# Where three products of the first double read their left operands, and when two weight chunks are loaded

## Chip, cores and metric

The kernel runs on one core of one Trainium2 chip. The metric is the device time of one execution in microseconds (us). Everything is in 32-bit floats.

## What is computed

The input `x` is 4 batches of 1024 tokens with 1024 features. A self-attention layer with 16 heads of 64 is applied with a residual, and then a causal convolution over tokens with 4 taps, also with a residual. Cut to what matters:

```python
scale, shift = split(emb @ W_emb + b_emb)
xn = rms_norm(x, g_norm) * (1 + scale) + shift
q, k, v = heads(xn @ W_qkv)                 # 1024 x 3072 weights
q, k = rms_norm(q, g_q), rms_norm(k, g_k)
o = softmax(q @ k.T / 8) @ v                # per head
x = x + o + o @ W_out
x = x + causal_conv(x, taps=cond) + b       # 4 taps per feature
```

## The kernel before

**Products.** `xn @ W_qkv` is the work around the change. It is computed as 2 by 2 block products with seven multiplications in place of eight (a Strassen scheme). The left blocks are the two token halves by the two feature halves of `xn`, A11, A12, A21, A22, and four sums of them: S1 = A21 + A22, S2 = S1 - A11, S3 = A11 - A21, S4 = A12 - S2. The right blocks are two head pairs' weights by feature halves and four differences T1 to T4. The products are named P1 (A11), P2 (A12), P6 (S2, T2), P7 (S3, T3), P4 (A22, T4), P5 (S1, T1) and P3 (S4). One run of the scheme serves two head pairs and is called a `Double`; there are 4 per batch, 16 in all. Each of its seven products has four token tiles `t` = 0 to 3 of 128 tokens, so a double has 28 pieces (`piece`, L634). A piece is four matmuls over `k` = 0 to 3 into one PSUM tile, followed by adds on VectorE (DVE) or a copy on ScalarE (ACT). The PSUM tiles come from a pool of three (`ps_m`, tag "m"), which transposes share.

**Left operands.** A left operand is needed transposed: features on partitions. `Chunk` (L259) makes all of them for one feature block `k` and one token quarter `q` (tiles 0, 1 for q = 0 and tiles 2, 3 for q = 1): transposes on TensorE, scale and shift on ACT or DVE, the four sums on DVE (`sums`, L318, records at L321). They stand in one or several SBUF tiles, reached by `self.r(place)`, and `store` (L336, records at L338) writes them to a DRAM scratch `scrA[b][q]`. A product reads its operand back with `load_a` (L610, records at L620) into one of three buffers of tag "a". For batch 0 the eight chunks' tiles lie in SBUF room that other things use later (`R_HOMES`, L249): the second quarter's `k` = 1 in the pool "x", and its `k` = 2 and 3 in the two tiles of the pool "ob".

**The first double.** P1 and P2 of the first double get their operands from `direct` (L622) and the first of the chunks are made meanwhile. Its order of pieces is `FIRST_PRODUCTS` (L573): P1 and P2 on all tiles, then P6, P7, P4 on tiles 0 and 1 (pieces 8 to 13), P6, P7, P4 on tiles 2 and 3 (pieces 14 to 19), P5 (20 to 23), P3 (24 to 27). For tiles 0 and 1, `load_a` returns at once and `piece` takes the operand from the chunk's own tiles; for tiles 2 and 3 it is read back from `scrA`.

**Right operands.** `Weights` (L524) loads four blocks of `W_qkv` for one `k` into one tile of the pool "ob" (or elsewhere for the first double), makes the differences (`combine`, L553, records at L561: GpSimd for the first double, DVE later) and stores them to the DRAM scratch `scrB` (L562). They are made once, in batch 0. `STEPS_B` (L1084) says at which pieces of a double the four chunks of the next double are loaded; the first tuple is that of the first double. For the second double's chunks 0 and 1 the differences follow 12 us after the load on the kernel's own clock (`TO_B`), for later ones in a gap. `load_w` (L592) fetches a product's right operand, from `scrB` (L604) or from `W_qkv` (L601), into one of three buffers of tag "w".

**Order of the work.** TensorE (PE), DVE, ACT and GpSimd run their instructions in the order in which the program gives them: `piece`, `tick` and `defer` keep a clock of estimated times and put deferred steps where it says. The DMAs are all issued by SyncE (SP), whose order is made by the framework's scheduler. An SP issue that must wait, for a buffer or for data, holds those behind it.

Of the kernel before, what the change touches and what calls it, by code (L numbers as in the profile page):

```python
# [15 lines left out]
P = 128  # L16
# [5 lines left out]
def kernel(  # L22
# [42 lines left out]
    KH = NJ // 2  # L65
# [33 lines left out]
    def flush(due):  # L99
        while True:  # L100
            ready = [e for e in pending if due(e)]
            if not ready:
                return
            entry = min(ready, key=lambda e: e[:2])
            pending.remove(entry)
            entry[3]()

    def tick(us):

        clock[0] += us  # L110
        flush(lambda e: e[0] <= clock[0])
# [28 lines left out]
    def need(*key):  # L140
        flush(lambda e: e[2] == key)
# [440 lines left out]
    class Double:  # L582
# [26 lines left out]

        def load_a(self, i):  # L610

            _, place, t = self.products[2 * i]
            if (place, t // 2) in self.a or self.n == 0 and t < 2:
                return
            for k in range(KH):
                if self.b == 0:
                    need("s", t // 2, k)
                need("r", self.b, t // 2, k)
            a = self.a[place, t // 2] = self.tile_a(place, t // 2)
            nc.sync.dma_start(a, scrA[self.b][t // 2][:, place])  # L620
# [13 lines left out]
        def piece(self, i):  # L634

            name, place, t = self.products[i]
            px, py = self.pairs
            pm = ps_m.tile([P, 512], F32, tag="m", name=f"pqkv_{self.n}_{name}_{t}")[:, :W3]
            w, a = self.w[name], self.a.get((place, t // 2))
            for k in range(KH):  # L640
                if a is None:
                    need("s", 0, k)
                nc.tensor.matmul(  # L643
                    pm,
                    (chunks[0, k].r(place) if a is None else a[:, k, :])[:, t % 2 * P : (t % 2 + 1) * P],
                    w[:, k, :],
                    start=(k == 0),
                    stop=(k == KH - 1),
                )
            tick(TIME)  # L650
            if name == "P1":
                self.u2[t] = apool.tile([P, W3], F32, tag="u2", name=f"u2_{self.n}_{t}", bufs=HT)
                nc.scalar.copy(self.u2[t], pm)
            elif name == "P6":
                nc.vector.tensor_add(self.u2[t], self.u2[t], pm)
            elif name == "P7":
                self.u3[t] = apool.tile([P, W3], F32, tag="u3", name=f"u3_{self.n}_{t}", bufs=HT)
                nc.vector.tensor_add(self.u3[t], self.u2[t], pm)
            else:
                pr, g, u = {"P2": (px, 0, self.u2), "P4": (px, 1, self.u3), "P5": (py, 1, self.u3), "P3": (py, 0, self.u2)}[name]  # L660
                for dst, at in pr.parts(g * HT + t):
                    nc.vector.tensor_add(dst, u[t][:, at], pm[:, at])  # L662
                if name == "P5":
                    nc.vector.tensor_add(self.u2[t], self.u2[t], pm)
            if t == HT - 1 and name in ENDS:
                c, g = ENDS[name]
                self.pairs[c].done(g)
# [413 lines left out]
    STORE = 30.0  # L1081
    TO_B = 12.0
    P6_AT = 3
    STEPS_B = ((14, 17, 22, 25), (7, 12, 17, 22))  # L1084
    outs, norms, chunks, weights, doubles, quads = {}, {}, {}, {}, {}, {}
    LAST = (B - 1) * 2 * NJ
    NB = 2 * NJ
# [4 lines left out]
    def piece(T):  # L1092
# [17 lines left out]
        if T % 2 == 0 and 4 <= a < ND * NPR // 2:  # L1110
            free(lambda: load_a(a))
# [8 lines left out]
        if n < ND:  # L1120
# [18 lines left out]

            if b == 0 and d + 1 < PB and i in STEPS_B[d > 0]:  # L1140
                free(lambda: Weights(d + 1, STEPS_B[d > 0].index(i)).load())

# [87 lines left out]
    def between(p):  # L1230

        b, i = divmod(p, NB)
        slots = [[] for _ in range(7)]
        for j in range(7):
            T = 7 * (p + 4) + j
            slots[j] = piece(T) if T < ND * NPR + 16 else []
        slots[0].append((0.0, lambda: store(AGE)))
        d, k = divmod(p - 11, NB)
        if 0 <= d < B - 1 and k % 2 == 0 and k < NJ:
            slots[0].append((0.0, lambda: OutSums(d, k // 2).load()))  # L1240
        for a, g in enumerate(range(products_until(p), products_until(p + 1))):
            slots[(2, 5)[a]] += out_product(g)
        if p in REST_PLAN:
            at = sum(n for q, n in REST_PLAN.items() if q < p)
            for m in REST[at : at + REST_PLAN[p]]:
                slots[6] += [(0.0, lambda: store(AGE_REST))] + out_pieces(m)
                slots[6].append((0.0, lambda m=m: late.append((clock[0], outs[m].store))))
        return [piece for slot in slots for piece in slot]
# [59 lines left out]
    for T in range(NPR):  # L1308
        for step in START.get(T, ()):
            step()  # L1310
        run(piece(T))
# [87 lines left out]
```

## Time and profile before

| | |
|---|---|
| time, median of 3 runs | 2877.23 us (2870.78 to 2878.03) |
| profiled execution | 2868.63 us |
| its span, first to last instruction | 2866.9 us |
| mean granted TensorE clock | 0.995 |
| PE busy | 2766.6 us |
| DVE busy | 2183.8 us |
| ACT busy | 1689.7 us |
| DMA | 510.98 MB, 178 GB/s on the mean |

The times of rows are those of one profiled execution, counted from its first instruction. Rows of PE are matmuls (PEld the weight loads beside them); one matmul of the program is two records. "Idle before" is the engine's idle time ahead of a row with what ended it. The granted clock is the share of full speed that TensorE was given. DMA rows named SPq are the issues, not the transfers.

The first 140 us hold the start: embedding, the first operands and the first double. Attention begins with the scores of unit 0 at 136.8 us; from then on pieces of the next doubles are spread between the attention's units.

### The profile page before, as it was taken

The page shows a single profiled execution, that of the slowest core. Times are in us where ns is not written, and L with a number is a line of the kernel's source. Part 1 is how long each engine was busy: PE and PEld are TensorE (multiplying, and loading weights), DVE is VectorE, ACT ScalarE, POOL GpSimd, SP SyncE. Part 2 cuts the span into 40 slices and gives each one's busy share as a digit, 9 for nine tenths or more (in the row PEclk, how much of TensorE's full clock was granted, in tenths as well). Part 3 has the DMA queues.
Part 4 walks back from the last instruction along what each step waited for, and adds up shares of the span by engine and source line. Part 5 has one row for each costly group of instructions (what it writes and reads, how often), then busy time and mean ns, then how long its engine had stood idle before and what let it go on. Part 6 is the DMA issues. An engine that isn't in the chain of part 4 may idle for free.

```text
span 2866.9 us, 32127 instructions
## 1 busy us (share of the span) xinstructions
PE 2766.6 (97%) x10581; PEld 1310.3 (46%) x10581; DVE 2183.8 (76%) x2648; ACT 1689.7 (59%) x2278; POOL 1347.7 (47%) x534
## 2 busy tenths in 40 slices
PE   6999989999999999999999999999999999999898
PEld 3544444444444444454444444444444444444344
DVE  4488878888888777787878777777787868787863
ACT  4166757765656667764655667666565656565532
POOL 2055555565554553544554554454454455545520
PEclk9999999999999999999999999999999999999999
DMA  9954555645554565764565455675565435533333
GB/s 321 292 169 144 186 163 168 217 160 181 169 170 157 195 192 181 232 207 162 180 221 168 167 191 176 219 233 171 168 220 191 144 132 170 166 104 100 118 107 118
DMA packets 417277, 510.98 MB, mean 178 GB/s; under 512 B 40864, under 2 KB 326872, under 8 KB 407384
## 3 DMA queue, kind: packets, MB, share of 16 engines
q1 hardware_dynamic: 417112, 508.93, 54.5%
q8 instruction: 85, 1.39, 0.2%
q14 instruction: 80, 0.66, 0.1%
HBM read 413.43 MB, written 95.40 MB: 177 GB/s over the span
## 4 chain that ended last, share of the span: by engine, by line
PE 72%; DVE 13%; DMA 5%; ACT 4%; issue 3%; POOL 2%; SPq 1%; DVEq 0%; ACTq 0%; POOLq 0%
PE pqkv_P L643 28%; PE s L683 14%; PE pav L746 14%; PE po L1004 5%; PE po_P L935 4%; DVE mx L700 4%; PE po L935 3%; DVE sp L719 3%; DVE r L321 1%; POOL sum L725 1%; ACT sp L691 1%; PE qkt L502 1%; PE tot L761 1%; ACT sp L723 1%; DMA rec<-scrR 1%
## 5 line engine op out<-in xcount | busy, mean ns | idle before, releaser
L643 PE MATMUL pqkv_P<-w_P,a 128*128 128x384 f32 x3504 | 1193.0, 491 | 33.3 <-issue 10.1
L725 POOL TENSOR_TENSOR sum<-sum,sp 128x1024 f32<-128x1024 f32 x384 | 958.2, 2495 | 64.9 <-ACT sp L723 34.3
L643 PEld LDWEIGHTS pqkv_P<-w_P,a 128*128 128x128 f32 x3504 | 650.0, 191 | 507.1 <-issue 94.1
L691 ACT COPY sp<-s 128x1024 f32<-128x1024 f32 x512 | 506.2, 1016 | 461.8 <-PE s L683 415.2
L700 DVE TENSOR_TENSOR mx<-mx,sp 128x1024 f32<-128x1024 f32 x384 | 516.6, 1345 | 155.2 <-ACT sp L691 127.7
L719 DVE TENSOR_TENSOR sp<-sp,mbp 128x1024 f32<-128x1024 f32 x512 | 603.7, 1209 | 18.3 <-ACT mbp L714 18.0
L723 ACT ACTIVATE sp<-sp 128x1024 f32<-128x1024 f32 x512 | 526.7, 1054 | 140.2 <-DVE sp L719 136.3
L705 POOL PARTITION_ALL_REDUCE mb<-mx x64 | 220.5, 3446 | 817.8 <-DVE mx L700 618.0
L683 PE MATMUL s<-qT,kT 64*128 64x512 f32 x2048 | 514.1, 618 | 20.0 <-DVE sp L719 12.8
L746 PE MATMUL pav<-sp,v 128*64 128x512 f32 x2048 | 482.7, 603 | 0.0
L725 POOL TENSOR_TENSOR sum<-sp,sp 128x1024 f32<-128x1024 f32 x64 | 151.4, 2366 | 484.3 <-ACT sp L723 232.5
L683 PEld LDWEIGHTS s<-qT,kT 64*128 64x128 f32 x2048 | 174.6, 186 | 312.8 <-issue 202.9
L1040 DVE SCALAR_TENSOR_TENSOR y<-x,cols,y 128x512 f32<-128x512 f32 x192 | 248.3, 1298 | 48.4 <-ACT y L1028 43.8
L746 PEld LDWEIGHTS pav<-sp,v 128*64 128x64 f32 x2048 | 130.4, 136 | 327.2 <-issue 318.7
L700 DVE TENSOR_TENSOR mx<-sp,sp 128x1024 f32<-128x1024 f32 x64 | 107.8, 1685 | 104.1 <-ACT sp L691 104.0
L662 DVE TENSOR_TENSOR qk<-u,pqkv_P 128x256 f32<-128x256 f32 x256 | 106.0, 414 | 78.3 <-PE pqkv_P L643 76.9
L1004 PE MATMUL po<-ob,wo 128*128 128x512 f32 x352 | 155.1, 592 | 0.0
L935 PE MATMUL po_P<-o_P,wq_P 128*128 128x512 f32 x320 | 144.0, 592 | 0.4 <-DVE sp L719 0.4
L714 ACT COPY mbp<-mb 128x1024 f32<-128x1024 f32 x64 | 65.1, 1018 | 115.9 <-POOL mb L705 115.9
L494 DVE TENSOR_TENSOR qk<-qk,ms 128x1024 f32<-128x1024 f32 x64 | 126.4, 1975 | 2.2
L935 PE MATMUL po<-o_P,wq_P 128*128 128x512 f32 x240 | 108.0, 592 | 0.0
L480 ACT ACTIVATE sq<-qk 128x512 f32<-128x512 f32 x128 | 76.8, 628 | 51.0 <-DVE qk L662 51.0
(97 smaller groups left out, 1864.6 us busy)
## 6 DMA issues: line engine op xcount, KB each, us to landing
a<-scrA SPq DMA_DIRECT2D x215, 512.0 KB
w_P<-scrB SPq DMA_DIRECT2D x64, 768.0 KB
o_P<-scrS SPq DMA_DIRECT2D x40, 1024.0 KB
w_P<-in_L_cond_W_qkv_dram SPq DMA_DIRECT2D x192, 192.0 KB
o_P<-scrO SPq DMA_DIRECT2D x30, 1024.0 KB
scrA<-r SPq DMA_DIRECT2D x28, 896.0 KB
wq_P<-scrW SPq DMA_DIRECT2D x70, 256.0 KB
xc<-in_x_dram SPq DMA_DIRECT2D x64, 256.0 KB
```

What stands on the lines that cost most here:

```text
L643: nc.tensor.matmul(pm, (chunks[0, k].r(place) if a is None else a[:, k, :])[:, t % 2 * P : (t % 2 + 1) * P], w[:, k, :], start=(k == 0), s ...
L683: nc.tensor.matmul(ps[:, h, :], pr.kT[kt // HT][h * D : (h + 1) * D, kt % HT * P : (kt % HT + 1) * P], pr.qT[self.half][h * D : (h + 1) * ...
L691: nc.scalar.copy(sp, ps)
L700: nc.vector.tensor_max(self.mx, self.mx if kt > 1 else self.sp[0], self.sp[kt])
L705: nc.gpsimd.partition_all_reduce(self.mb.rearrange("p h q -> p (h q)"), self.mx.rearrange("p h q -> p (h q)"), P, bass_isa.ReduceOp.max,)
L719: nc.vector.tensor_sub(self.sp[kt], self.sp[kt], self.mb)
L723: nc.scalar.activation(sp, sp, AF.Exp)
L725: nc.gpsimd.tensor_tensor(self.sum, self.sum if kt > 1 else self.sp[0], sp, ALU.add)
L746: nc.tensor.matmul(self.pav[h * D : (h + 1) * D, :], self.pr.v[kt // HT][:, kt % HT, h * D : (h + 1) * D], self.sp[kt][:, h, :], start=(kt ...
L935: nc.tensor.matmul(pm, self.w[name][:, k, :], self.o[name][:, k, :], start=(k == 0 and name not in ("P2", "P3", "P4")), stop=(k == KH - 1),)
L1004: nc.tensor.matmul(self.pm, self.w[kh][:, k % KH, :], oTs[b, k, half], start=False, stop=(k == NJ - 1),)
L1040: nc.vector.scalar_tensor_tensor(self.y, self.x1[:, k : k + HN], cols[:, r : r + 1], self.y, ALU.mult, ALU.add)
```

## The change

Three edits. `load_a` also returns at once, in the first double, for P6, P7 and P4 on any tile. `piece` then takes the operand from the chunk of the tile's own quarter, `chunks[0, t // 2 * KH + k]` (KH is 4), and asks that the sums of that quarter have been given. `STEPS_B` loads chunks 0 and 1 of the second double at pieces 18 and 20 of the first in place of 14 and 17. P5 and P3 on tiles 2 and 3 still read from `scrA`.

```diff
         def load_a(self, i):
-            _, place, t = self.products[2 * i]
-            if (place, t // 2) in self.a or self.n == 0 and t < 2:
+            name, place, t = self.products[2 * i]
+            if (place, t // 2) in self.a or self.n == 0 and (t < 2 or name in ("P6", "P7", "P4")):
                 return
...
             for k in range(KH):
+                chunk = chunks.get((0, t // 2 * KH + k))
                 if a is None:
-                    need("s", 0, k)
+                    need("s", t // 2, k)
                 nc.tensor.matmul(
                     pm,
-                    (chunks[0, k].r(place) if a is None else a[:, k, :])[:, t % 2 * P : (t % 2 + 1) * P],
+                    (chunk.r(place) if a is None else a[:, k, :])[:, t % 2 * P : (t % 2 + 1) * P],
...
-    STEPS_B = ((14, 17, 22, 25), (7, 12, 17, 22))
+    STEPS_B = ((18, 20, 22, 25), (7, 12, 17, 22))
```

## Prediction

> **What bounds the kernel now.** I read the page's busy shares and chain first, then the waits of TensorE (PE), then the timeline of the stretch that the change touches.
>
> ```profile
> PE 2766.6 (97%) x10581; PEld 1310.3 (46%) x10581; DVE 2183.8 (76%) x2648; ACT 1689.7 (59%) x2278; POOL 1347.7 (47%) x534
> ...
> PE 72%; DVE 13%; DMA 5%; ACT 4%; issue 3%; POOL 2%; SPq 1%; DVEq 0%; ACTq 0%; POOLq 0%
> ```
>
> PE is busy 97% of the span and holds 72% of the chain, so only two things can shorten the run: PE work taken out, or PE idle time. The change takes no matmul out. Of the 100 us of PE idle, the page's waits name one that the change aims at: 5.2 us, once, for a transfer `a<-scrA`. The chain in order of time shows what made it:
>
> ```profile
> 84.74 5.74 DMA scrA<-r
> 90.50 5.23 DMA a<-scrA
> 95.86 13.47 PE pqkv_P L643 x32
> ```
>
> The last store of the second quarter's operands is issued at 84.74 and lands at about 90.5; only then may the read of the same data go out, and it is another 5.23 us before PE starts at 95.86. The timeline of PE around it (start, length, then idle before in brackets):
>
> ```profile
> 77.43 13.20 PE L643 MATMUL pqkv_P<-w_P,r 128*128 128x384 f32 x40
> 95.86 13.47 PE L643 MATMUL pqkv_P<-w_P,a 128*128 128x384 f32 x32 [5.23 <-DMA a<-scrA]
> 109.17 0.60 PE L502 MATMUL qkt<-ident,qk 128*128 128x128 f32 x4
> ...
> 145.52 10.59 PE L643 MATMUL pqkv_P<-w_P,a 128*128 128x384 f32 x32
> 155.94 0.60 PE L502 MATMUL qkt<-ident,qk 128*128 128x128 f32 x4
> ```
>
> A product of one token tile is 8 of these records. Both x32 rows are four products, yet one takes 13.47 us and the other 10.59. The stretches say why (columns: length, busy time of PE, weight load, DVE, ACT, POOL, then granted PE clock, DMA share, GB/s):
>
> ```profile
> 91.50:94.90 3.40, 0.00 (x0) 0.00 (x0) 0.00 (x0) 0.00 (x0) 0.00 (x0) 1.00 0.88 293
> 94.90:98.30 3.40, 2.44 (x4) 1.52 (x5) 0.00 (x0) 0.00 (x0) 0.00 (x0) 0.50 0.98 284
> 98.30:101.70 3.40, 3.40 (x6) 1.69 (x5) 0.34 (x1) 0.00 (x0) 0.00 (x0) 0.50 1.07 364
> 101.70:105.00 3.30, 3.30 (x12) 1.92 (x11) 0.77 (x2) 0.00 (x0) 0.00 (x0) 0.99 0.32 103
> ```
>
> After the empty stretch PE got half its clock from 94.9 to 101.7. The wait costs its idle time and a slow restart.
>
> **Part 1: the three reads of the second quarter go; the products read the tiles where they were made.** The operands are made by DVE at L321; its last one before these products ends at 84.7, and the products' weights (P6, P7, P4) are already in use for the first quarter. So P6 on token tile 2 needs nothing that is late. It would start where the fifth product after 77.43 ends. Two products take 5.16 us start to start (115.21 to 120.37), one 2.58; five of the x40 row give 77.43 + 13.20 less the row's 0.16 of overlap (5.32 against 5.16) = 90.47. Idle removed: 95.86 - 90.47 = 5.39 us.
> Slow restart removed: start to start the slow four take 109.17 - 95.86 = 13.31, the normal four 155.94 - 145.52 = 10.42; 2.89 us. [...] Here two windows were granted half clock, of which PE ran 101.7 - 95.86 = 5.84 us, half of it lost = 2.9. [...]
> The reads themselves (3 x 512 KB) also leave the DMA engines, which are at a share of 0.9 to 1.0 there. That gain is not counted: what comes later is tested below for being in time.
>
> **Part 2: the queue of SP.** The list of the built program shows the order: after the second quarter's last store come at once the three stores of the first quarter that stood at 92.42, then the reads of S1 and S4 for the second quarter (for P5 and P3), then P5's weights, the first operand of the second double, P3's weights, and only then chunk 0 and chunk 1 of the second double, each four reads. Those two chunks are written into tiles that the change now keeps in use until P4 on tile 3, so SP waits there for PE, with the second double's P1 weights, the next batch's x and the second double's P2 weights behind it. Before:
>
> ```profile
> 87.66 1.95 SPq L546 DMA_DIRECT2D b<-in_L_cond_W_qkv_dram  x3
> 90.50 1.29 SPq L620 DMA_DIRECT2D a<-scrA  x3
> ...
> 92.42 3.28 SPq L338 DMA_DIRECT2D scrA<-r  x3
> ...
> 104.20 0.34 SPq L604 DMA_DIRECT2D w_P<-scrB  x1
> ```
>
> P5's weights go out when P6 on tile 3 frees their buffer: before 104.20 for a use at 115.21; now 90.47 + 5.16 = 95.6 for a use at 106.9. The same 11 us; nothing. S1's read goes out at 90.5 behind 1.3 MB of stores and is used at 112.1; at 300 GB/s that is some 6 us; nothing. P1's weights of the second double waited for P4's buffer before as well and are used 30 us later; nothing.
> Chunk 0 goes out when P4 on tile 3 is nearly done, 90.47 + 6 x 2.58 + two transposes of 0.44 = 106.8; four issues at 0.62 end at 109.3. Landing: at best just behind the issue; at worst like the read at 90.50, which took 5.2 us under a full DMA load: 114.5. I take 112, since fewer transfers stand before it. Chunk 1 goes out behind P1's weights, 112 to 114.5, and lands by 119.7 at worst.
>
> **Part 3: DVE combines the two chunks later (L561).** The list puts chunk 0's four subtractions behind P5's second tile and the scaling of qk, in front of the adds of P5's third tile; chunk 1's behind P5's fourth tile. Durations as here:
>
> ```profile
> 118.99 2.32 DVE L561 TENSOR_TENSOR b<-b 128x384 f32<-128x384 f32 x4
> 121.23 0.41 DVE L662 TENSOR_TENSOR qk<-u,pqkv_P 128x256 f32<-128x256 f32 x1
> ```
>
> [...] So a late chunk holds up evictions. Walking it with all PE times 8.28 earlier: P5 tile 1 is evicted 112.3 to 113.3, reciprocal and scaling to 114.7, chunk 0 114.7 to 116.9 (it is there, at 112, at worst 114.5), P5 tiles 2 and 3 to 118.9, chunk 1 to 121.2, two reductions to 122.4, P3 tile 0 to 122.9. PE wants that PSUM tile back (three share the tag) at 131.12 - 8.28 = 122.8. A wait of about 0.1; bounds 0 and 1.0 (if each DVE row runs 5% longer). I take 0.1.
> From unit 0's scores on, the instruction lists of all compute engines are the same, so everything shifts as one. The next stop of PE, 2.85 us before 159.39, comes from DVE's rows behind the scores (chunks 2 and 3 among them) and shifts with it.
>
> **Sum.** -5.39 - 2.89 + 0.1 = -8.2 us. The profiled execution took 2868.6 us with a span of 2866.9; it would take 2860.4. It lies 8.6 below the median of the runs; the same 8.2 off the median gives 2869.0.
>
> **Rivals.**
> (a) More than that. The runs spread from 2870.8 to 2878.0 and the profiled one is below all; a wait on a store and a read at full DMA load is a place where an execution can lose more than 5.2 us, and without it that loss goes too. Also the half clock after the stop at 159.39 (1.9 us: 4.51 for one product) hangs on where the window falls. Against it: no row shows where the slower runs lose. It would give 10 to 16 less: about 2864.
> (b) Partly given back. P3's tile waits for the full 1.0 and chunk 0 lands some us late, or the shifted windows of the clock cost a second slow restart of 2.9. It would leave 2 to 6: about 2873.
> (c) Slower. One mechanism: chunk 0 is not there when DVE reaches it at 114.7. DVE stands, P5's adds behind it wait, PE runs out of PSUM tiles, us for us, and a stop of over 2.7 us adds a slow restart of 2.9. Landing at 120.0 uses up the gain; landing at 128.6 gives 2886, slower by 0.3%. For it: reads at 0.62 us each in one queue behind a wait for PE, and DMA shares of 0.9 to 1.0 between 80 and 140. Against it: even the 5.2 us read is in time by 0.2.
> That the change doesn't act can be left out: the list of PE reads r tiles in all six products.
>
> **How the numbers follow.** Full gain carried through 0.55 (2866 to 2872); (a) 0.25; (b) 0.09; (c) 0.11. A measurement of this kernel can tell about 0.3%, 8.6 us, from no change; the likeliest case lies at its edge, so half of it (0.28) counts as faster. Faster 0.28 + 0.25 = 0.53; within 0.27 + 0.09 = 0.36; slower 0.11. Range 2861 to 2875: all of the likeliest, most of (a) and (b).
>
> **What would show it.** Right: PE goes from r to r at about 90.5 with no idle time, the granted clock stays 1.00 from 80 to 120, six products take 16.4 us with their transposes, unit 0's scores begin at about 128.6 (before 136.82), and the shift is still 8 us at 1000 us. Part 3 right: L561 at about 114.7 and 118.9 without idle time before it, and PE's wait before P3's third tile under 1 us. Wrong: an idle DVE before L561, PE waiting for DVE there, a slow restart at another place, or a shift that fades where DVE sets the pace (180 to 860 us).

## The result and the profile after

The changed kernel took 2864.91 us (median of 6 runs, 2860.03 to 2866.47), the kernel before 2876.0 us (median of 6, 2870.48 to 2878.03). The ratio is 0.9962, with a 95% interval of 0.9948 to 0.9975: 0.38% or 11 us faster, forecast 8.2 us (0.29%). A second measurement of the same kernel, below, gave 0.9974 (0.9962 to 0.9986). The mean of the two is 9.2 us.

The page of the changed kernel (one execution of 2866.47 us, span 2864.7, clock 0.993), its busy times and the shares of the chain:

```profile
PE 2768.9 (97%) x10581; PEld 1312.7 (46%) x10581; DVE 2187.2 (76%) x2648; ACT 1689.6 (59%) x2278; POOL 1347.5 (47%) x534
...
PE 75%; DVE 11%; ACT 4%; DMA 4%; issue 2%; POOL 2%; SPq 1%; DVEq 0%; POOLq 0%; ACTq 0%
```

The instructions of the compute engines are as many as before. PE is busy 2.3 us longer (2768.9 against 2766.6), although a slow restart is gone; the section on the second trace of the kernel before comes back to that. Its share of the chain rose from 72% to 75%, and that of the DMAs fell from 5% to 4%. The chain in order of time (start, length) no longer has the store and the read in it:

```profile
78.30 23.35 PE pqkv_P L644 x72
101.65 0.44 PE qkt L502 x4
102.09 2.58 PE pqkv_P L644 x8
```

The timeline of PE around the change (start, length, then idle before in brackets):

```profile
78.14 23.52 PE L644 MATMUL pqkv_P<-w_P,r 128*128 128x384 f32 x72
101.49 0.60 PE L502 MATMUL qkt<-ident,qk 128*128 128x128 f32 x4
101.92 2.75 PE L644 MATMUL pqkv_P<-w_P,r 128*128 128x384 f32 x8
...
123.69 2.82 PE L644 MATMUL pqkv_P<-w_P,a 128*128 128x384 f32 x8
...
129.45 1.99 PE L684 MATMUL s<-qT,kT 64*128 64x512 f32 x8
```

Nine products run from one `r` tile to the next without a stop: 72 records in 23.52 us, where before there were 40, a stop and 32. From the start of this row to unit 0's scores it is 129.45 - 78.14 = 51.31 us; before, with the scores at

```profile
136.82 1.99 PE L683 MATMUL s<-qT,kT 64*128 64x512 f32 x8
```

it was 136.82 - 77.43 = 59.39. The difference, 8.08 us, is what the change does in this stretch; forecast 8.2. The granted clock in the stretch (columns: length, busy time of PE, weight load, DVE, ACT, POOL, then granted PE clock, DMA share, GB/s) is whole. The kernel before first, then the changed one:

```profile
80.00:100.00 20.00, 14.77 (x40) 8.16 (x39) 7.11 (x18) 0.00 (x0) 0.00 (x0) 0.87 0.96 321
```

```profile
80.00:100.00 20.00, 20.00 (x63) 11.64 (x63) 9.47 (x21) 0.00 (x0) 0.00 (x0) 1.00 0.93 320
100.00:120.00 20.00, 20.00 (x69) 12.06 (x68) 11.09 (x26) 4.00 (x7) 0.00 (x0) 1.00 0.85 259
```

SP's queue and the two chunks' differences on DVE went as walked:

```profile
96.52 0.32 SPq L604 DMA_DIRECT2D w_P<-scrB  x1
...
107.08 2.54 SPq L546 DMA_DIRECT2D b<-in_L_cond_W_qkv_dram  x4
109.71 2.56 SPq L601 DMA_DIRECT2D w_P<-in_L_cond_W_qkv_dram  x4
112.31 2.62 SPq L546 DMA_DIRECT2D b<-in_L_cond_W_qkv_dram  x4
```

```profile
115.31 2.33 DVE L561 TENSOR_TENSOR b<-b 128x384 f32<-128x384 f32 x4
117.56 0.41 DVE L663 TENSOR_TENSOR qk<-u,pqkv_P 128x256 f32<-128x256 f32 x1
...
119.54 2.33 DVE L561 TENSOR_TENSOR b<-b 128x384 f32<-128x384 f32 x4
```

No idle time stands ahead of either L561 row: both chunks had landed.

One thing does not fit at first sight. The two profiled executions differ by only 2.2 us in span (2866.9 and 2864.7), and instance by instance the lead shrinks: 7.4 us at the first maximum of unit 0, 4.3 at 400 us, 1.5 from 800 to 1000 us, 3.3 behind 2000 us. The prediction had named such a fading lead as a sign against it. The experiments had to settle that as well.

### The profile page after: what moved, and what is told of

It reads as the page before. It is cut to its first block, busy times and chain, and to the rows that moved or that the text cites. A ratio compares the mean times of both kernels' runs of the same rounds, so it can differ in the third digit from the quotient of the medians.

```text
span 2864.7 us, 32127 instructions
## 1 busy us (share of the span) xinstructions
PE 2768.9 (97%) x10581; PEld 1312.7 (46%) x10581; DVE 2187.2 (76%) x2648; ACT 1689.6 (59%) x2278; POOL 1347.5 (47%) x534
## 4 chain that ended last, share of the span: by engine, by line
PE 75%; DVE 11%; ACT 4%; DMA 4%; issue 2%; POOL 2%; SPq 1%; DVEq 0%; POOLq 0%; ACTq 0%
PE pqkv_P L644 30%; PE s L684 15%; PE pav L747 14%; PE po L1005 5%; PE po_P L936 4%; PE po L936 3%; DVE mx L701 3%; DVE sp L720 2%; POOL sum L726 1%; PE qkt L502 1%; PE tot L762 1%; ACT sp L724 1%; ACT sp L692 1%; DMA scrR<-few 1%; PE po L991 1%
## 5 line engine op out<-in xcount | busy, mean ns | idle before, releaser
L644 PE MATMUL pqkv_P<-w_P,a 128*128 128x384 f32 x3456 | 1176.4, 491 | 28.8 <-issue 10.7
L644 PEld LDWEIGHTS pqkv_P<-w_P,a 128*128 128x128 f32 x3456 | 640.5, 191 | 496.0 <-issue 87.5
L701 DVE TENSOR_TENSOR mx<-mx,sp 128x1024 f32<-128x1024 f32 x384 | 514.3, 1339 | 156.4 <-ACT sp L692 128.9
L701 DVE TENSOR_TENSOR mx<-sp,sp 128x1024 f32<-128x1024 f32 x64 | 116.0, 1813 | 103.5 <-ACT sp L692 103.5
```

The source lines that it names most:

```text
L644: nc.tensor.matmul(pm, (chunk.r(place) if a is None else a[:, k, :])[:, t % 2 * P : (t % 2 + 1) * P], w[:, k, :], start=(k == 0), stop=(k ...
L701: nc.vector.tensor_max(self.mx, self.mx if kt > 1 else self.sp[0], self.sp[kt])
```

## The experiments

Three questions: is the gain what the sum says it is (a stop and its slow restart) or something else that the change did; what keeps the moved chunks from costing anything; and where the lead went in the profiled pair. The table puts the two readings side by side. "Row to scores" is taken from each trace as above; the ratio is to runs of the kernel before made beside it, with its 95% interval. The ratios are those on record. Plain medians of the same runs can differ from them by 0.1% (0.9962 for e7, 2865.44 of 8 runs against 2876.35 of 49, and 0.9976 for e1), so differences between ratios in the third decimal are not to be read closely.

| kernel | row starts | scores of unit 0 | row to scores | ratio |
|---|---|---|---|---|
| before | 77.43 | 136.82 | 59.39 | |
| before, second trace (e8) | 77.47 | 136.76 | 59.29 | |
| before + later loads (e1) | 75.46 | 133.06 | 57.60 | 0.9989 (0.9978 to 1.0) |
| before + filler (e2) | 77.71 | 133.78 | 56.07 | 0.999 (0.9982 to 0.9998) |
| changed | 78.14 | 129.45 | 51.31 | 0.9962 (0.9948 to 0.9975) |
| changed, again (e7) | 77.63 | 128.95 | 51.32 | 0.9974 (0.9962 to 0.9986) |
| changed + unused reads (e3) | 77.11 | 128.43 | 51.32 | 0.9974 (0.9964 to 0.9984) |
| P6 alone (e4) | 75.92 | 127.68 | 51.76 | 0.9973 (0.9963 to 0.9983) |
| changed, no time to land (e5) | 76.72 | 136.95 | 60.23 | 1.0 (0.9989 to 1.0012) |
| changed + chunk 2 earlier (e6) | 77.94 | 129.26 | 51.32 | 0.9963 (0.9949 to 0.9977) |
| the same + filler at the start (e9) | 77.57 | 128.89 | 51.32 | 0.9963 (0.9949 to 0.9978) |

**The changed kernel again**

No edit: the changed kernel as it is, beside new runs of the kernel before.

> The changed kernel unaltered, timed again beside the kernel before. Theory (one stop of 5.4 us and one slow restart of 2.9 us are gone, everything else shifts; executions of either kernel differ by how many windows of 3.4 us at half clock they meet by chance): 8 us less at equal mean granted clock, and within each kernel 1 thousandth of mean clock is worth about 2.87 us. A second profile has the stop after the scores of unit 0 again, but half-clock windows at other places than the first. Rival (the gain fades for good where DVE sets the pace, as the first pair of profiles suggests: 7.4 us ahead at 140 us, 1.5 at 800): about 2 us less at equal clock, and the windows at 431, 544 and 704 us come again.

Median 2865.44 us (8 runs), ratio 0.9974. The stretch took the same 51.32 us. Its span was 2862.0, 4.9 below that of the first profile of before. Of the first trace's half-clock windows (3.41 us at a granted clock of 0.50) at 431, 544 and 704 us two came again (429 and 702), which the expectation had given to its rival. But e1 and e2 below, which keep the stop, have the last of them too (707 and 709), so it is not a price of the change. Runs can also be set side by side at the same mean granted clock. Over 92 runs of before and 48 of the kernels that have no stop before P6 (changed, e7, e3, e4), the mean times are:

| mean clock | before | without the stop |
|---|---|---|
| 0.990 | 2879.1 (7) | 2876.1 (2) |
| 0.992 | 2875.5 (22 runs) | 2868.6 (10) |
| 0.993 | 2873.0 (23) | 2866.8 (9) |
| 0.994 | 2871.9 (14) | 2864.8 (14) |
| 0.995 | 2868.6 (6) | 2863.0 (13) |

From 0.992 to 0.995 the gain at equal clock is 5.6 to 7.1 us, and 3.0 at 0.990, where there are only two runs without the stop (and none at 0.991). A line fitted to each group, with one slope for both, gives 6.3 us with a standard error of 0.5. That rules out the rival's 2 us, but the expectation of 8 us missed: it had left out that the slow restart is a loss of clock and drops out of such a comparison, so that the idle time alone (5.39) should remain. The clock is where the rest shows: its mean over these runs is 0.9924 before and 0.9935 without the stop, 0.0011 more, and two half-clock windows of 3.41 us less would be 0.0012. On the plain means the gain is 8.6 us (2874.6 to 2866.0). So over many runs neither part is lost on the way to the end. Per 0.001 of clock a run of before is 2.1 us longer. If PE had work through all of every half-clock window it would be 2.87 by estimate (0.1% of the run), so by this slope, which is a correlation, a window at half clock is estimated to cost about three quarters of its full price.

**The slow restart by itself**

The kernel before, with 44 transposes of the identity into a spare PSUM tile ahead of P6 on tile 2: work for PE over the stop, so that there is a wait but no idle PE.

```diff
+            if self.n == 0 and i == 14:
+                warm = ps_m.tile([P, 512], F32, tag="m", name="warm")
+                for _ in range(44):
+                    nc.tensor.transpose(warm[:, :P], ident, ident)
```

> The kernel before, with 44 transposes of the identity into a spare PSUM tile ahead of P6 on tile 2, so that PE is busy during the wait for the read; nothing is left out. It prices the slow restart alone. Theory: the read still ends PE's real wait at about 95.9 us, but the four products after it take 10.4 us in place of 13.3: 2.9 less than before. [...] If the half clock had another cause than the idle time: 0 and 13.3 again.

PE's timeline of this kernel:

```profile
90.74 4.97 PE L641 MATMUL warm<-ident 128*128 128x128 f32 x44
95.74 10.56 PE L647 MATMUL pqkv_P<-w_P,a 128*128 128x384 f32 x32
106.13 0.60 PE L502 MATMUL qkt<-ident,qk 128*128 128x128 f32 x4
```

The wait is still there: the read lands at 95.60 by the trace's record, and PE starts on it 0.14 us later, as in the kernel before (95.73 and 95.86). The filler covers it, and the four products behind it take 10.56 us in place of 13.47: 2.91 us, against 2.89 in the sum. The rest of the 3.3 us in the table is a read that came 0.4 us sooner after the row's start. The runs agree: 0.10% of 2876 us is 2.9 us, with an interval of 0.6 to 5.2. At equal clock nothing significant is left of it (0.6 us, standard error 0.7, by the same fit), as it should be for something that saves clock alone. So in this trace the wait cost 5.4 us of idle time and 2.9 us of clock.

**The later loads alone**

```diff
-    STEPS_B = ((14, 17, 22, 25), (7, 12, 17, 22))
+    STEPS_B = ((18, 20, 22, 25), (7, 12, 17, 22))
```

> The kernel before with the new load steps alone (chunks 0 and 1 at pieces 18 and 20); the three products read from DRAM as before. Theory: no gain, the wait and the restart stay; in this program's order two of the three stores of the first quarter (0.9 MB) come ahead of the reads, which at 350 GB/s puts PE's start about 2.5 us later: 0 to 3 us slower than before. Rival (the later loads relieve the DMA engines and make the read quicker): the wait falls from 5.2 to 3 or 4 us, 2 us faster.

```profile
75.46 13.19 PE L643 MATMUL pqkv_P<-w_P,r 128*128 128x384 f32 x40
93.06 12.19 PE L643 MATMUL pqkv_P<-w_P,a 128*128 128x384 f32 x32 [4.40 <-DMA a<-scrA]
```

The expectation of a longer wait missed. The wait became shorter, 4.40 us, and the four products took 12.19. SP's queue shows one difference: in the kernel before, three of chunk 0's reads are issued at 87.66, ahead of the operand's read at 90.50, and here all of them come behind it, at 90.04 after 88.21. From the read's issue to PE's start it is 4.85 us here and 5.36 before. But in e2, with three of those reads ahead of it as before, it is 3.87 us (91.87 to 95.74), so the order of the reads is not shown to be the cause. The stretch is 1.8 us shorter. Most of that, 1.28 us, is the cheaper restart: PE came back 0.1 us into a half-clock window (from 92.94) and paid for that one alone (clock 0.51 from 92.9 to 96.3, 0.99 in the 3.40 us after it), and where a stop falls against these windows is not the loads' doing as far as is shown. The runs have 0.11% (0 to 0.22%) by the ratio and 2.9 us at equal clock (standard error 0.9), so the loads alone may well shorten the wait; by what is open. It is no further gain in the changed kernel: it is a shorter form of the stop that the changed kernel doesn't have at all. The other half alone, the reads gone with the chunks loaded as before, was not tried: the chunks' tiles are then still in use.

**Does it help that the reads leave the DMA engines?**

The changed kernel, which still issues the three reads of the second quarter but uses none of them.

```diff
-            if (place, t // 2) in self.a or self.n == 0 and (t < 2 or name in ("P6", "P7", "P4")):
+            if (place, t // 2) in self.a or self.n == 0 and t < 2:
                 return
...
-            a = self.a[place, t // 2] = self.tile_a(place, t // 2)
+            a = self.tile_a(place, t // 2)
             nc.sync.dma_start(a, scrA[self.b][t // 2][:, place])
+            if not (self.n == 0 and name in ("P6", "P7", "P4")):
+                self.a[place, t // 2] = a
```

> The changed kernel, with the three reads of 512 KB issued all the same into their buffers, and used by nobody. Theory: PE does not wait for them, so as the changed kernel within 1 us: no idle time at 90 us, unit 0's scores at about 129 us. Rival (part of the gain comes from 1.5 MB less on the DMA engines): P5's operand or weights arrive late by up to 4 us and PE stops before P5's third tile, at about 113 us.

```profile
77.11 23.51 PE L646 MATMUL pqkv_P<-w_P,r 128*128 128x384 f32 x72
...
128.43 1.99 PE L686 MATMUL s<-qT,kT 64*128 64x512 f32 x8
```

51.32 us, and a ratio of 0.9974, that of the second measurement of the changed kernel. The page has the three reads again (215 reads of this kind, 212 in the changed kernel). The 1.5 MB less of transfers are worth nothing that shows; the gain is that PE need not wait for them.

**Is it the first of the three products, or all three?**

```diff
-            if (place, t // 2) in self.a or self.n == 0 and (t < 2 or name in ("P6", "P7", "P4")):
+            if (place, t // 2) in self.a or self.n == 0 and (t < 2 or name == "P6"):
```

> The changed kernel with only P6 taking the second quarter's operand where it is made; P7 and P4 read theirs from DRAM as before. Theory (what counts is that the first product after the store does not wait): the read of S3 goes out when P6's third tile starts and takes 4.7 to 5.2 us, P6's two tiles take 5.16, so PE idles 0 to 0.5 us and the clock stays whole: 8 us faster than before, as the changed kernel. Rival (all three reads had to go): PE stops 2 us or more before P7's third tile at about 95.6 us and restarts slowly, which leaves 3 to 5 us.

```profile
75.92 18.36 PE L644 MATMUL pqkv_P<-w_P,r 128*128 128x384 f32 x56
94.47 5.40 PE L644 MATMUL pqkv_P<-w_P,a 128*128 128x384 f32 x16 [0.20 <-DMA a<-scrA]
```

P7 waits 0.20 us for its read, and the stretch takes 51.76 us, 0.44 more than in the changed kernel; the ratio is 0.9973. The first product alone holds the gain. P6's two products of 5.16 us are long enough to cover nearly all of P7's read, and PE does not wait for P4's.

**What the cover of the moved chunks is worth**

The changed kernel, with 5 us on the kernel's own clock in place of 12 between a chunk's load and its differences. Chunk 0's load is not moved; DVE comes to L561 sooner.

```diff
-    TO_B = 12.0
+    TO_B = 5.0
```

> The changed kernel, with the subtractions of chunks 0 and 1 given 5 us behind their loads on the kernel's clock in place of 12. In DVE's list chunk 0's now stand ahead of the add of P4's fourth tile, whose matmuls free the chunk's room, so DVE has to stand until the chunk lands. It is the mechanism of the slower rival, forced. Theory: DVE idles from about 104.7 to 112 us, PE stops 2.5 us before P5's third tile and 0.8 before P3's first, with or without a slow restart of 1.6 to 1.9: unit 0's scores 3.4 to 5.3 us later than in the changed kernel, so 3 to 5 us faster than before remain. It also shows when the chunk lands: 112 us by the prediction, 114.5 at worst. Rival (late chunks are hidden): under 1 us later.

DVE's timeline, then PE's:

```profile
109.15 0.56 DVE L561 TENSOR_TENSOR b<-b 128x384 f32<-128x384 f32 x1 [5.23 <-DMA b<-in_L_cond_W_qkv_dram]
110.66 1.74 DVE L561 TENSOR_TENSOR b<-b 128x384 f32<-128x384 f32 x3 [0.95 <-DMA b<-in_L_cond_W_qkv_dram]
...
118.32 0.56 DVE L561 TENSOR_TENSOR b<-b 128x384 f32<-128x384 f32 x1 [3.15 <-DMA b<-in_L_cond_W_qkv_dram]
```

```profile
113.03 5.40 PE L644 MATMUL pqkv_P<-w_P,a 128*128 128x384 f32 x16 [1.59 <-issue]
122.61 8.38 PE L644 MATMUL pqkv_P<-w_P,r 128*128 128x384 f32 x16 [4.17 <-DVE u L665]
```

This is rival (c) made real. DVE stands before both chunks, the adds behind it wait, and PE stops twice: 1.59 + 4.17 us of idle time, and 3.06 us of slow restart in the second row (8.38 in place of 5.32). That is 8.8 of the 8.9 us by which the stretch is longer than in the changed kernel, and the whole gain is gone (ratio 1.0). The mechanism held, the size was under-rated: I had expected 3.4 to 5.3 us. Here chunk 0's last transfer landed at 110.57, 2.4 us behind the end of its issue (108.20), and DVE went on at 110.66. Chunk 1's landed at 119.72, 3.7 behind its issue (116.03), which itself came later than in the changed kernel, because stores of chunk 0's late differences stood ahead of it in SP's queue. In the changed kernel's own trace the last transfers land at 112.12 (the prediction took 112) and 117.76. DVE came there at 115.31 and 119.54: 3.2 us to spare for chunk 0, 1.8 for chunk 1.

**The next stop of PE**

In the changed kernel PE stops for 3.2 us ahead of 152.40, the one before 159.39 in the kernel before, and what is late there is DVE's chain, with the differences of chunks 2 and 3 in it. Here chunk 2's are made before unit 0's work, as those of 0 and 1 are.

```diff
-                if d > 1 or k > 1:
+                if d > 1 or k > 2:
```

> The changed kernel, with chunk 2's subtractions 12 us behind their load, ahead of unit 0, in place of the gap behind unit 0's maxima; a try for a faster version. Theory: in the gap DVE has only chunk 3 left, P2's adds come 2.2 us earlier or more, the stop of PE at about 149 us falls from 3.2 to 1 us and its slow restart of 1.9 us goes: 4 us less than the changed kernel at 170 us, ratio to before about 0.996 where the changed kernel has 0.997. Rival (the stop only moves, since DVE paces the units after): nothing is left of it at 300 us.

```profile
149.96 2.82 PE L644 MATMUL pqkv_P<-w_P,a 128*128 128x384 f32 x8 [0.97 <-PE qkt L502]
...
173.34 0.64 PE L762 MATMUL tot<-sum,ones 128*32 128x256 f32 x8 [1.89 <-POOL sum L726]
```

The stop fell to 0.97 us and kept the full clock, which put this trace 3.6 us ahead of the second one of the changed kernel at 164 us. At 201 us 0.4 of it was left: PE stopped for 1.89 us at 173 and got a half-clock window behind it. The stop moved. The ratio of 0.9963 can't be told from the changed kernel's.

**Filler at the start**

The kernel of the section above (e6), with transposes of the identity into a spare tile of the scores' pool over the two stops at 62 to 71 us.

```diff
+    def warm(n):
+        spare = ps_s.tile([P, 2, HN], F32, tag="s", name=f"warm_{n}")
+        for _ in range(n):
+            nc.tensor.transpose(spare[:, 0, :P], ident, ident)
...
-        8: [lambda: across(0, 1)],
+        8: [lambda: warm(26), lambda: across(0, 1), lambda: warm(22)],
```

> The changed kernel with chunk 2's combine ahead of unit 0 (as in e6_chunk2) and filler transposes of the identity in a spare tile: 26 ahead of the first double's start and 22 behind it, so that TensorE has work over its stops at 62.6 to 65.7 us (3.07) and 68 to 71 us (2.75). Theory (a stop costs more than its own length because the clock restarts at half): the first product's first eight matmuls take 2.7 us in place of 5.46 (changed kernel) or 4.5 (e6_chunk2), so unit 0's scores come 1.9 to 3 us earlier than in e6_chunk2; the median ratio to the kernel before goes from 0.9963 to 0.9955, with an interval that overlaps. Rival (the fillers run over into real work, or what unit 0 waits for is not TensorE): the scores come no earlier and the ratio stays at 0.9963 or above.

```profile
64.20 3.00 PE L1292 MATMUL warm<-ident 128*128 128x128 f32 x26
67.44 2.40 PE L307 MATMUL xtp<-ident,x 128*128 128x128 f32 x16 [0.24 <-DVE v L663]
69.67 2.56 PE L1292 MATMUL warm<-ident 128*128 128x128 f32 x22
72.58 2.82 PE L644 MATMUL pqkv_P<-w_P,r 128*128 128x384 f32 x8 [0.34 <-DMA w_P<-scrB]
```

P6's first product took 2.82 us in place of the 5.46 of the changed kernel's first trace, as the theory said, and the granted clock is 1.00 from 60 to 80 us. The 2.82 alone would prove little: e1 and e4 have it without filler (70.48 and 70.93 us), as their half-clock window fell earlier, on the transposes at 65 us (3.40 and 3.42 us there, 2.40 in e9). Unit 0's scores did not come the expected 1.9 to 3 us earlier, but 0.4: this execution was already 1.7 us behind e6 when it came to the filler (the product row before it ends at 64.4 and not at 62.7), which the filler can't have made. From there to the scores it gained 2.0. In the runs there is nothing to see: 0.9963, as e6. So it stays open whether the filler is worth 2 us of the whole.

**The kernel before, a second trace**

No edit. The question is why the lead shrank in the first pair of profiles.

> A second look at the kernel before, unaltered. Theory: the stop and the slow restart at 90 us again (5.2 and 2.9 us, the latter 1.6 where a single window falls on it); the first profile was a lucky one behind 170 us, with three windows of half clock where the five other profiles have 6 to 9 (counted in windows of 3.4 us), so this one has more of them and is longer, 2870 to 2876 us. Rival (the kernel before meets fewer windows by its nature, and the changed one loses part of its gain there for good): three or four windows again.

Its span was 2873.5, 6.6 us longer than the first trace of the same program. The stop is there again, and its slow restart of 13.57 - 10.59 = 2.98 us:

```profile
95.70 13.57 PE L643 MATMUL pqkv_P<-w_P,a 128*128 128x384 f32 x32 [5.03 <-DMA a<-scrA]
```

Until 163 us the two traces are equal within 0.1 us; by 440 us the second is 3.7 behind, by 750 us 6.8. Three stretches of the first trace, then of the second:

```profile
390.00:400.00 10.00, 8.16 (x34) 2.85 (x34) 5.30 (x8) 7.26 (x10) 9.69 (x5) 1.00 0.89 268
430.00:440.00 10.00, 7.88 (x34) 2.62 (x34) 7.19 (x10) 9.42 (x14) 8.84 (x4) 1.00 0.37 113
...
635.00:645.00 10.00, 10.00 (x46) 3.21 (x44) 6.41 (x3) 4.71 (x5) 9.13 (x4) 1.00 0.16 62
```

```profile
390.00:400.00 10.00, 8.15 (x26) 2.69 (x26) 4.00 (x7) 5.57 (x8) 9.69 (x5) 0.83 0.81 246
430.00:440.00 10.00, 7.45 (x22) 2.81 (x24) 6.34 (x10) 8.08 (x10) 8.15 (x4) 0.83 0.50 181
...
635.00:645.00 10.00, 8.16 (x30) 2.33 (x28) 4.77 (x5) 3.24 (x4) 9.69 (x5) 0.83 0.51 199
```

The second trace has one half-clock window in each of them, and the first has none. The profile shown of before was a lucky one, with one half-clock window between 165 and 2700 us (at 467) where its twin has five (at 395, 436, 638, and two in a row at 467). The first trace of the changed kernel has four there (431, 462, 544, 704), three more than the lucky one. At half of 3.41 us each that is up to 3 x 1.7 = 5.1 us, and the lead fell by 4.1; it is also why PE is busy longer in that trace. Set against the second trace of before, the second one of the changed kernel does not lose its lead: 7.8 us at unit 0, 8.8 at 445 us, 10.5 at 790, 11.8 at 2590. Set against the first it keeps 7.9, 6.3, 4.1 and 5.0. The fading depends on which execution of before is taken.

## Why the prediction was right

**What bounds the kernel.** PE at 97%, and one stop of it made by a store and a read back. Shown: e2 takes the slow restart away and leaves the wait, e4 takes away the one wait and gets all, and e3 gives the transfers back and loses nothing.

**Part 1.** Idle time 5.39 and restart 2.89, together 8.28; the stretch shows 8.08 with a small wait in it. The price of the restart was taken from the row, and it held (2.91 in e2, 2.98 in e8). It is not a fixed one, though: in e1 it was 1.60 us (12.19 against 10.59), with one window at half clock where before has two. In e1 PE starts 0.1 us into its first half-clock window, in before 0.95 us (94.91 to 95.86); that the price hangs on this is my estimate. The two traces of before have it at nearly the same place (half clock from 94.91 and from 94.95), so how often it is 2.9 and how often 1.6 is not known. Taking the one profile's price was in part luck.

**Part 2.** P5's weights were issued at 96.52 (95.6 forecast), chunk 0 at 107.08 (106.8), chunk 1 at 112.31 (112). The row starts at 78.14 and not 77.43, 0.7 of this. Chunk 0 landed at 112.12, the value taken, and chunk 1 at 117.76, 1.9 us inside the worst case of 119.7.

**Part 3.** L561 at 115.31 and 119.54 (114.7 and 118.9, again 0.6 later with the row) and no idle time before it. The wait of PE ahead of P3's third tile was 0.25 us, 0.1 forecast: DVE finished P3's first tile at 123.58 in place of 122.9, again with the row, and PE began at 123.69 in place of 123.44. Small, and inside its bounds of 0 to 1.0. That the adds wait behind L561 shows in before, where the add of P5's second product, done by about 120.5, begins at 121.23, when the four subtractions from 118.99 are through (2.32 us), and in e5, where DVE stood for 5.23 us and the add behind L561 began at 112.32.

**The sum** of -8.2 lies inside both measured intervals (-15.0 to -7.2, and -10.9 to -4.0). That the median came out at 2864.9 and not 2869.0 is 2.9 us of a larger ratio, which the interval doesn't tell from chance, and 1.2 us of the runs of before, whose median fell from 2877.23 to 2876.0.

**What the prediction had wrong.** "The shift is still 8 us at 1000 us" was read off as a test for one pair of profiles, and there it was 1.5. The step behind it, that from unit 0 on everything shifts as one, takes for granted that both executions get the same clock. They don't: the second trace of before ended 6.6 us later than the first, with four more half-clock windows, worth up to 6.8 us at half of 3.41 us each. The test can be made over many runs, or at equal clock, and not on a pair. A second slip did no harm: by its own worst case chunk 1 lands at 119.7, behind DVE's 118.9, so the rival of a late chunk had a way in of 0.8 us that the prediction does not mention.

**The rivals.** (a) asked for a wait that had often been longer than the profiled one. The first measurement, 11 us and 2864.9, taken alone would fit its 10 to 16 and its 2864. The mean of the two, 9.2, lies under that; the two traces of before show waits of 5.23 and 5.03 us; and the 6.3 us at equal clock leave about 0.9 for longer waits. So little speaks for it, though two traces can't exclude it. (b) did not come about at the places it named. One thing of its kind did: after the stop at 152.40 the first trace of the changed kernel got two half-clock windows (5.46 us for a product, before 4.51), 0.95 us, and in the second trace it got one (4.51). (c) is a true mechanism, and e5 shows its price. Its slow restart behind a stop of over 2.7 us is an estimate that did not hold: in before a product behind a stop of 2.74 us (70.75) and one behind 2.85 us (159.39) took 4.51 us, but in e1 one behind 3.22 us (156.01) took 2.82. The prediction told (c) for chunk 0 alone, which has 3.2 us to spare; chunk 1, with 1.8, is the one that would be late first.

## What to carry to other kernels

Here a wait of the bounding engine cost its idle time (5.39 us) and what the clock took afterwards (2.89 us); read the second from the same product's row elsewhere in the profile, and try filler work when the two have to be told apart. When operands are written out and read back, try the first consumer alone: once it has its data from where they were made, its own work may cover the reads of all the others, as P6's 5.16 us did in e4 but for 0.20. And before a gain under half a per cent is followed through one pair of profiles, compare the clock in both: a second profile of the kernel before is a cheap control.

## What the hardware showed that I had not expected

**Where TensorE's clock was at half, and for how long.** The traces give the granted clock in stretches. Up to 500 us, the first trace of before has it at 0.50 from 71.02, 94.91, 159.77 and 466.97 us, for 3.41, 6.83, 3.41 and 3.41 us. In the first trace of the changed kernel such a stretch lasts 3.41, 6.83 or (from 65.87) 10.24 us. A window is here a stretch of 3.41 us. Busy time of PE in the 3.40 us ahead of a half-clock window: 0.03 us (e5, 118.4), 0.55 (before, 156.4), 1.38 (changed, 147.8), 1.51 (e6, 170.7). One and the same stop, of 1.84 and 1.85 us at 393 us, in the two traces of the kernel before, window by window:

```profile
391.80:395.20 3.40, 1.56 (x6) 0.52 (x8) 2.38 (x4) 3.38 (x5) 3.32 (x2) 1.00 1.01 284
395.20:398.60 3.40, 3.40 (x18) 1.06 (x16) 2.24 (x6) 2.18 (x3) 3.24 (x3) 1.00 0.90 266
```

```profile
391.90:395.30 3.40, 1.55 (x8) 0.40 (x6) 1.97 (x3) 3.18 (x7) 3.32 (x2) 1.00 0.92 263
395.30:398.70 3.40, 3.40 (x8) 0.86 (x10) 2.03 (x5) 0.94 (x1) 3.32 (x2) 0.50 0.87 236
```

A window with 1.56 us of work was followed by full clock and one with 1.55 by half, so behind the same stop of under 2 us both came; busy time alone does not tell them apart. In before alone, the clock stayed at 1.00 behind a window with 1.41 us (385.05 to 388.45) and fell to 0.50 behind one with 2.08 (463.55 to 466.97). What decides is open. The mean clock goes with the spread of the runs (2865 to 2883 us in before; in the table above 2879.1 us on the mean at 0.990, 2868.6 at 0.995); how much of that spread comes from such stops is not shown. Half-clock windows in which PE was busy for 2.20 (changed, 151.2), 2.44 (before, 94.9), 2.59 (e5, 121.8) or 2.92 us (second trace of before, 467.0) were followed by another half one, and those with 3.24 (e1, 92.9) or 3.40 us (e7, 152.8) by a full one. So PE's restart 0.95 us into a window met two of them (before), and the one 0.1 us into it met one (e1). What the clock follows is not shown; busy time is what the profile has, and its ends are modelled.

**Identity transposes kept the clock.** With 44 of them over a stop of 5 us (e2, 90.7 to 95.8), and with 26 and 22 over the two at the start (e9, 60 to 80), the granted clock stayed at 1.00. Whether they would also bring back a clock that has fallen was not tried.
